# Head products of a graph network on TensorE: four blocks of 256 columns, or seven block products of 128

## The chip, the core and the metric

The kernel runs on one core of a Trainium2 chip. The core has five engines that run side by side, each through its own fixed list of instructions: TensorE (PE, matrix products, with a separate weight load, PEld), VectorE (DVE), ScalarE (ACT), GpSimd (POOL) and SyncE (SP, which here issues every DMA). Data sits in SBUF, 128 partitions wide. Products land in PSUM, which has 8 banks, each with room for 512 f32 numbers in each partition. [...]what TensorE computes is taken out by ACT or DVE. The metric is the device time of one execution in microseconds: the median of three runs.

## The reference

There are 128 graphs of 64 nodes, each node with 512 features in f32, and one adjacency matrix. Four layers follow, each adding its result to x and normalizing over the features:

```
x = layernorm(x + L0(x))    # deg*(x Wi^T + b) + adj x Wj^T
x = layernorm(x + L1(x))    # 4 attention heads, elu; output attention with W_out, elu; FFN; layernorm
x = layernorm(x + L2(x))    # one attention: softmax(mask(leaky(e_src + e_dst))) (x W2)
x = layernorm(x + L3(x))    # the same with W3
```

A head computes `attn (x W_h)`, with W_h of 512 x 512; the kernel uses that it equals `(attn x) W_h`. Layers 2 and 3 are done in the same way. All products are in f32.

## The kernel before

**Tiling.** The 8192 tokens (nodes of all graphs) are taken 256 at a time: 32 "pairs" p of T = 2 token tiles of 128 tokens, and a token tile holds two graphs. For each pair, Python generators write out the stages: `stage_first` (layer 0), `stage_scores` (attention weights of the heads, and y = attn x for each head, transposed, by half-height matmuls named yp), `stage_heads` (y W_h, elu, kept as hT), `stage_project` (hT W_out, named who), `stage_out` (output attention, elu, FFN, layer norm), and `stage_gat` twice (layers 2 and 3).

**The order.** A queue at the end of the kernel (lines 1081 to 1113) gives each stage a due time in units of `TURN` = 107 us per pair and advances the generators by the times that they yield. That gives each step a rank. `Plan.order` (lines 205 to 297) then makes a list schedule from a cost per instruction (`cost`, line 317) with waits between engines, and plays it out: each engine gets a fixed order of instructions (all issued at line 304, so the profile names line 304 for nearly everything). A tile pool has a fixed number of buffers per tag; a step that opens a tile waits until a buffer of the tag is free. All PSUM tiles share one tag of 8 buffers, one bank each. `with nc.soon()` puts what empties PSUM ahead of other work.

**Products.** Layer 0 (from pair 4 on), the projection, the second FFN matrix and layers 2, 3 use `strassen` (line 586): a 2 x 2 block product with seven block products in place of eight. Its left blocks (tokens, two token tiles by two halves of the contraction) are the stationary operand, the right blocks (weights, 256 columns) move. Sums of left blocks are made on POOL (`sums`, line 649). Sums of right blocks are made once: for layer 0 and W_out they are stored in DRAM and each block is loaded for each use (`stage_stream`, `part_from`, a ring "ws" of 4 buffers of 512 KB); for w2, W2 and W3 all seven blocks stay in SBUF (`stage_resident`, line 560). Two PSUM tiles, stx and sty, take the results in turn; DVE adds them to the result. At most two such units run at a time (line 593).

The heads do not use it. For each head, four output blocks of 128 features: the weight block is stationary, and all 256 tokens of the pair move:

```
hp[:, c, :, :], lhsT=w_h[h][:, k, ts(2 * q + c, P)],
rhs=y[:, k, h % 2, :, :].rearrange("p t i -> p (t i)"),
```

Two output blocks share a PSUM bank, and `elu` (line 772) takes the bank out by two ACT operations and one on DVE.

**Layers 2 and 3.** The products of attention and x, transposed (gp, line 1042), use half-height matmuls: for each graph 64 tokens are the contraction, x is stationary and the 64 columns of its attention move. ACT and DVE then bring the results into gT, with one sum.

**Scores.** The head scores of pair 0 are made on TensorE (transposed x, then the products fp with the score weights); for other pairs DVE makes them by dot products with rows that DMAs spread over the partitions.

Of the kernel before, what the change touches and what calls it, by code (L numbers as in the profile page):

```python
# [28 lines left out]
NWS = 4  # L29
AHEAD = 4  # L30
# [286 lines left out]
def cost(engine, name, args, kw, out):  # L317

    size = max(math.prod(v.shape[1:]) for v in out) if out and isinstance(out[0], View) else 512
    if engine == "tensor":  # L320
        if name == "transpose":
            return size * 0.00085, 0.0

        beside = P * P // math.prod(kw["lhsT"].shape)
        return size * (0.00169, 0.00106, 0.0, 0.00053)[beside - 1], 0.0
# [10 lines left out]
def gnn_stack_kernel(  # L336
# [124 lines left out]

    was = {}
    score = {}

    def score_weights(Ws, avecs, name):
# [3 lines left out]
        for h in range(n):  # L469
            for s in range(2):  # L470
                for c in range(KC):
# [4 lines left out]
                    )  # L476
            yield 5.0
# [15 lines left out]
    for p in range(1, AHEAD):  # L493
        xs[p] = load_x(p)
    w_h, a_h = [], []
    for h in range(H):
        w_h.append(weight(W_heads[h], D, f"wh{h}"))
        a_h.append(
            rows([a_heads[h, ts(s, D)] for s in range(2)], f"a_{h}", ["who", "o", "A", "A"][h])
        )  # L500
    beta_sb = row(beta, "beta")
# [6 lines left out]
    PARTS = ("21", "11", "T1", "T2", "22", "T3", "T4")  # L508

    def sums_of(parts, b12):  # L510

        add = lambda out, a, b, op: nc.gpsimd.tensor_tensor(out, a, b, op)
        add(parts["T1"], b12, parts["11"], ALU.subtract)
        add(parts["T2"], parts["22"], parts["T1"], ALU.subtract)
        add(parts["T3"], parts["22"], b12, ALU.subtract)
        if "T4" not in parts:
            parts["T4"] = parts["11"]
        add(parts["T4"], parts["21"], parts["T2"], ALU.subtract)
# [3 lines left out]
    def stage_stream(src, name):  # L522

        parts = {}
        for q in ("11", "12", "21", "22"):
            i, j = int(q[0]) - 1, int(q[1]) - 1
            parts[q] = unit.tile([P, KC, D // 2], FP, tag="ws", bufs=NWS, name=f"raw_{name}_{q}")
            nc.sync.dma_start(
                out=parts[q],
                in_=src[ts(i, D), ts(j, D // 2)].rearrange("(c p) o -> p c o", p=P),  # L530
# [4 lines left out]
        def store(q):  # L535
            d[q] = dp.tile([P, KC, D // 2], FP, tag=f"d_{name}_{q}", name=f"d_{name}_{q}")
            nc.sync.dma_start(out=d[q], in_=parts[q])
# [3 lines left out]
        parts["T1"] = unit.tile([P, KC, D // 2], FP, tag="who", name=f"T1_{name}")  # L541
        parts["T2"] = unit.tile([P, KC, D // 2], FP, tag="o", name=f"T2_{name}")
        parts["T3"] = parts["12"]
        sums_of(parts, parts["12"])
        for q in ("T1", "T2", "T3", "T4"):
            store(q)
# [3 lines left out]
    def part_from(name, p):  # L550

        def part(q):
            t = unit.tile([P, KC, D // 2], FP, tag="ws", bufs=NWS, name=f"ws_{name}_{p}_{q}")
# [3 lines left out]

    resident = {}

    def stage_resident(src, name):  # L560

        w = wp.tile([P, len(PARTS), KC // 2, D // 2], FP, tag=f"r_{name}", name=f"r_{name}")
        parts = {q: w[:, i, :, :] for i, q in enumerate(PARTS)}
        b12 = unit.tile([P, KC // 2, D // 2], FP, tag="s3", bufs=2, name=f"b12_{name}")
        for q in ("11", "12", "21", "22"):
            i, j = int(q[0]) - 1, int(q[1]) - 1
            nc.sync.dma_start(
                out=b12 if q == "12" else parts[q],
                in_=src[ts(i, D // 2), ts(j, D // 2)].rearrange("(c p) o -> p c o", p=P),
            )  # L570
        yield 4.0
        sums_of(parts, b12)
        resident[name] = lambda q: parts[q]
        yield 0.0
# [11 lines left out]
    def strassen(A, B, S, R, kc, name, gap, fresh=False, whole=lambda t: None):  # L586
# [6 lines left out]
        while no >= 2 and no - 2 not in ended:  # L593
            yield 1.0
        s1, s2, s3, s4 = S(name)
        R = R.rearrange("p t (h o) -> p (t h) o", h=2)
        half = D // 2
        x = psum.tile([P, half], FP, tag="b", name=f"stx_{name}")
        yz = psum.tile([P, 2, half], FP, tag="b", name=f"sty_{name}")

        def product(ps, a, q, first, last):
            b = B(q)
            with nc.together():
                for k in range(kc):
                    nc.tensor.matmul(
                        ps, lhsT=a[:, k, :], rhs=b[:, k, :], start=(first and k == 0),
                        stop=(last and k == kc - 1), skip_group_check=True,
                    )
# [12 lines left out]
        product(yz[:, 0, :], A(1, 0), "21", True, False)  # L621
        yield gap
        product(x, A(0, 0), "11", True, False)
        put(x, R[:, 0, :])
        yield gap
        s4(A(1, 0))
        product(yz[:, 1, :], s1, "T1", False, False)
        if fresh:
            add(yz[:, 0, :], R[:, 0, :])
            put(yz[:, 1, :], R[:, 3, :])  # L630
        else:
            add(yz, R[:, 0:4:3, :])
        yield gap
        product(x, s2, "T2", False, False)
        put(x, R[:, 1, :])
        yield gap
        product(yz[:, 1, :], A(1, 0), "22", False, True)
        add(yz[:, 1, :], R[:, 1, :])
        whole(0)
        yield gap  # L640
        product(x, s3, "T3", False, False)
        add(x, R[:, 3, :])
        yield 2 * gap
        product(x, A(1, 1), "T4", False, True)
        put(x, R[:, 2, :])
        whole(1)
        ended.add(no)

# [129 lines left out]


# [4 lines left out]
    outs = {}  # L784
# [381 lines left out]
```

## Time and profile before

| | |
|---|---|
| median of three runs | 3453.69 us (3453.62 to 3456.76) |
| the profiled execution: time, and span from first to last instruction | 3457.33 us, 3455.5 us |
| mean granted TensorE clock | 0.987 |
| PE, PEld, DVE, ACT, POOL busy | 3381.8, 2878.7, 2424.6, 997.7, 1444.6 us |
| moved by DMA | 540 MB, 156 GB/s in the mean, 47.3% of the 16 DMA engines |
| costliest group on PE: head products hp | 4096 records, 951.8 us busy |

How to read the profile's lines. A group line names the line of the code, engine, operation, the tiles (written<-read, numbers left out), partitions x elements, the count, then busy time, mean ns of one, and idle time of the engine before it with what ended it. In a timeline line the first number is the start in us from the span's start, the second the length to the last end, and consecutive equal instructions are merged (x8). For matmuls the pair "128*128 128x256" gives the stationary block and what is moved through it. An f32 matmul appears as two records, a transposition as one. Matmuls overlap: a record lasts longer than the distance to the next one, so the sum of records is not the work. The chain that ended last is followed back from the last instruction through what released each one.

### The profile page before, as it was taken

To read this page: it belongs to the slowest core of one execution; us is meant where nothing else is said; L and a number is where in the kernel's file an instruction comes from. 1 tells how busy PE (TensorE), PEld (TensorE's weight loads), DVE (VectorE), ACT (ScalarE), POOL (GpSimd) and SP (SyncE) were. 2 spreads that over 40 slices of the span, in tenths; PEclk is the share of its full clock that TensorE was granted. 3 is DMA by queue.
4 is the path that set the end of the run, shared out by engine and by line. 5 is a ranking of instruction groups with operands and counts; after the bars stand their busy time and mean duration, and the time that the engine had idled before them with its cause. 6 is when DMAs were issued, how large, how long until landed. Compare 5 with 4: busy or idle time off the path is not lost.

```text
span 3455.5 us, 52610 instructions
## 1 busy us (share of the span) xinstructions
PE 3381.8 (98%) x19228; PEld 2878.7 (83%) x19228; DVE 2424.6 (70%) x5408; ACT 997.7 (29%) x2536; POOL 1444.6 (42%) x1528
## 2 busy tenths in 40 slices
PE   8899999999999999999999999999999999999986
PEld 4788888888888888888888888888888888888875
DVE  7757766777667777677777677777677777677755
ACT  1233223232233232233232233232232232232221
POOL 5424344444344444344444344444344444344322
PEclk9999999999999999999999999999999999999987
DMA  8834444444454444444445454445444445444420
GB/s 310 269 110 141 159 154 151 153 159 160 154 169 147 158 159 159 153 165 149 159 156 165 150 166 146 160 155 167 154 159 152 156 153 169 153 158 147 136 87 31
DMA packets 203761, 540.38 MB, mean 156 GB/s; under 512 B 21824, under 2 KB 31088, under 8 KB 203504
## 3 DMA queue, kind: packets, MB, share of 16 engines
q1 hardware_dynamic: 203504, 537.02, 47.3%
q8 instruction: 154, 2.52, 0.3%
q14 instruction: 103, 0.84, 0.1%
HBM read 509.12 MB, written 27.81 MB: 155 GB/s over the span
## 4 chain that ended last, share of the span: by engine, by line
PE 94%; DVE 4%; POOL 1%; issue 1%; DMA 1%; ACT 0%; SPq 0%; POOLq 0%; ACTq 0%; DVEq 0%
PE hp L304 25%; PE stx_o L304 13%; PE stx L304 12%; PE sty_o L304 10%; PE sty L304 9%; PE hidp L304 7%; PE gp L304 4%; PE yp L304 3%; PE stx_y L304 3%; PE sty_y L304 2%; PE axp L304 2%; PE bc L304 1%; PE op L304 1%; DVE x L304 1%; PE oTp L304 1%
## 5 line engine op out<-in xcount | busy, mean ns | idle before, releaser
L304 PE MATMUL hp<-ys,wh 128*128 128x256 f32 x4096 | 951.8, 381 | 0.0
L304 PEld LDWEIGHTS hp<-ys,wh 128*128 128x128 f32 x4096 | 765.2, 190 | 109.2 <-issue 2.1
L304 DVE CUSTOM_DVE_ANT_0 j<-x,rows 128x512 bf16<-128x512 f32 x752 | 613.8, 816 | 76.6 <-DMA rows<-d_h 66.5
L304 ACT ACTIVATE hT<-hp 128x512 f32<-128x512 f32 x256 | 152.5, 596 | 866.1 <-PE hp L304 865.7
L304 POOL TENSOR_SCALAR rs<-mv 128x1 f32<-128x1 f32 x256 | 104.5, 408 | 620.5 <-DVE mv L304 591.2
L304 DVE TENSOR_SCALAR x<-x,mv,rs 128x512 f32<-128x512 f32 x256 | 213.2, 833 | 106.5 <-POOL rs L304 106.4
L304 DVE SCALAR_TENSOR_TENSOR hT<-hT,hp 128x512 f32<-128x512 f32 x256 | 175.1, 684 | 143.7 <-ACT hT L304 139.6
L304 DVE TENSOR_TENSOR x<-stx,x 128x256 f32<-128x256 f32 x368 | 154.9, 421 | 156.1 <-PE stx L304 152.7
L304 PE MATMUL sty_o<-ws_wo,hT 128*128 128x256 f32 x1024 | 247.7, 385 | 1.4 <-DMA ws_wo<-d_wo 1.4
L304 PE MATMUL stx_o<-ws_wo_T,s_o 128*128 128x256 f32 x1024 | 245.7, 383 | 2.8 <-DVE e L304 2.1
L304 PE MATMUL hidp<-oT,w 128*128 128x256 f32 x1024 | 237.6, 382 | 0.7 <-ACT oT L304 0.7
L304 PEld LDWEIGHTS sty_o<-ws_wo,hT 128*128 128x128 f32 x1024 | 189.6, 190 | 51.4 <-issue 22.3
L304 PEld LDWEIGHTS stx_o<-ws_wo_T,s_o 128*128 128x128 f32 x1024 | 192.3, 190 | 31.6 <-DVE e L304 2.5
L304 PEld LDWEIGHTS hidp<-oT,w 128*128 128x128 f32 x1024 | 190.1, 190 | 28.8 <-ACT oT L304 0.9
L304 PE MATMUL sty<-r_W,gT 128*128 128x256 f32 x768 | 202.2, 387 | 1.7 <-ACT gT L304 1.7
L304 ACT COPY ys<-yp 128x512 f32<-128x512 f32 x256 | 131.7, 600 | 176.4 <-PE yp L304 171.6
L304 DVE BATCH_NORM_STATS2 st<-x 128x6 f32<-128x512 f32 x256 | 176.8, 691 | 6.4
L304 DVE TENSOR_TENSOR who<-stx_o,who 128x256 f32<-128x256 f32 x160 | 66.9, 418 | 156.2 <-PE stx_o L304 156.1
L304 POOL TENSOR_TENSOR rs<-rs,mhalf 128x1 f32<-128x1 f32 x256 | 160.8, 628 | 21.3
L304 PEld LDWEIGHTS sty<-r_W,gT 128*128 128x128 f32 x768 | 148.5, 194 | 23.9 <-ACT gT L304 2.4
L304 ACT ACTIVATE hT<-hT 128x512 f32<-128x512 f32 x256 | 161.4, 630 | 8.2
L304 POOL TENSOR_TENSOR hid<-hid 128x256 f32<-128x256 f32 x32 | 32.2, 1005 | 306.3 <-ACT hid L304 299.8
(170 smaller groups left out, 6225.3 us busy)
## 6 DMA issues: line engine op xcount, KB each, us to landing
ws_wo_T<-d_wo_T SPq DMA_DIRECT2D x256, 512.0 KB, 3.4
ws_wo<-d_wo SPq DMA_DIRECT2D x192, 512.0 KB, 3.4
rows<-d_h SPq DMA_DIRECT2D x248, 256.0 KB, 4.2
ws_w_T<-d_w_T SPq DMA_DIRECT2D x112, 512.0 KB, 3.3
ws_w<-d_w SPq DMA_DIRECT2D x84, 512.0 KB, 3.1
rows<-d SPq DMA_DIRECT2D x128, 256.0 KB, 3.9
rows_1o<-in_a_out_dram SPq DMA_DIRECT2D x64, 256.0 KB, 3.4
out_dram<-x SPq DMA_DIRECT2D x64, 256.0 KB, 2.0
```

Source lines behind the costliest of these rows:

```text
L304: getattr(getattr(self.tc.nc, s.engine), name)(*map(real, args), **{k: real(v) for k, v in kw.items()})
```

## The change

**Heads.** A general `seven` is split out of `strassen`: the schedule of the seven block products and of emptying PSUM, with the block product itself handed in. `strassen` uses it as before. The heads now use it too, with weight blocks stationary and token blocks moving: the 512 x 512 head matrix is cut into 2 x 2 blocks of 256 x 256, the result likewise into two halves of features by two token tiles. Each block product is 4 matmuls with a stationary 128 x 128 block and 128 columns moving. Sums of weight blocks are made once at the start, in place in SBUF (`head_sums`); sums of token blocks on POOL after each y tile (t1, t2, and one in place), and one per head (`t4`). The results are copied out by ACT (four per head) and added by DVE (three per head) into hT, and then `elu_of` applies the elu to each half of hT, with a PSUM tile as scratch. Up to `UNITS` = 3 units of seven products run at a time.

**Weights.** The seven blocks of w2, W2 and W3 are no longer kept in SBUF: they are stored in DRAM at the start and loaded for each use, through a ring "wk" of 6 buffers of 256 KB. The seven blocks of layer 0 are prepared later than before.

**Layers 2 and 3.** The attention of a token tile is written into a tile aTg of 128 x 128 with zeros between the two graphs (two such tiles, filled with zeros once), so that gp becomes full-height matmuls with 128 columns moving, one PSUM tile per token tile.

**Scores.** Pair 1 makes its head scores on TensorE as pair 0 does. The planner's cost of half-height matmuls is changed.

```diff
+NWK = 6
+UNITS = 3
...
-        return size * (0.00169, 0.00106, 0.0, 0.00053)[beside - 1], 0.0
+        return (
+            size * 0.00169 if beside == 1 else 0.208 / beside + 0.0003 * size
+        ), 0.0
...
+    aTg = [cp.tile([P, T, P], FP, tag=f"aTg{i}", name=f"aTg{i}") for i in range(2)]
+    for aT in aTg:
+        nc.gpsimd.memset(aT, 0.0)
...
+        w = wp.tile([P, KC // 2, 7, D // 2], FP, tag=f"wh{h}", name=f"wh{h}")
...
+    RINGS = {D: ("ws", NWS), D // 2: ("wk", NWK)}
+
+    def head_sums(w):
+
+        a11, a21, a12, a22, s2, s3, s4 = (w[:, :, i, :] for i in range(7))
+        nc.gpsimd.tensor_tensor(a21, a21, a22, ALU.add)
+        nc.gpsimd.tensor_tensor(s2, a21, a11, ALU.subtract)
+        nc.gpsimd.tensor_tensor(s3, a22, s2, ALU.subtract)
+        nc.gpsimd.tensor_tensor(s4, a12, s2, ALU.subtract)
...
+    def part_from(name, p, K=D):
+
+        ring, bufs = RINGS[K]
 
         def part(q):
-            t = unit.tile([P, KC, D // 2], FP, tag="ws", bufs=NWS, name=f"ws_{name}_{p}_{q}")
+            t = unit.tile([P, K // P, D // 2], FP, tag=ring, bufs=bufs, name=f"ws_{name}_{p}_{q}")
             nc.sync.dma_start(out=t, in_=streams[name][q])
             return t
         return part
-
-    resident = {}
-
-    def stage_resident(src, name):
...
+    def seven(product, R, shape, name, gap, fresh=False, once=lambda: None, whole=lambda t: None):
...
-        while no >= 2 and no - 2 not in ended:
+        while no >= UNITS and no - UNITS not in ended:
             yield 1.0
+        x = psum.tile([P, *shape], FP, tag="b", name=f"stx_{name}")
+        yz = psum.tile([P, 2, *shape], FP, tag="b", name=f"sty_{name}")
+        y, z = yz[:, 0], yz[:, 1]
...
+        product(0, y, True, False)
+        yield gap
+        product(1, x, True, False)
+        put(x, R(0, 0))
+        yield gap
+        once()
+        product(2, z, False, False)
+        if fresh:
+            add(y, R(0, 0))
+            put(z, R(1, 1))
+        else:
+            add(yz, R(None, None))
+        yield gap
+        product(3, x, False, False)
+        put(x, R(0, 1))
+        yield gap
+        product(4, z, False, True)
+        add(z, R(0, 1))
+        whole(0)
+        yield gap
+        product(5, x, False, False)
+        add(x, R(1, 1))
+        yield 2 * gap
+        product(6, x, False, True)
+        put(x, R(1, 0))
+        whole(1)
+        ended.add(no)
...
+    def elu_of(x, name):
+
+        ps = psum.tile(x.shape, FP, tag="b", name=f"elu_{name}")
+        with nc.soon():
+            nc.scalar.activation(ps, x, AF.Relu, scale=-1.0)
+            nc.scalar.activation(ps, ps, AF.Exp, scale=-1.0)
+            nc.vector.scalar_tensor_tensor(x, ps, -1.0, x, ALU.add, ALU.max)
...
-        if p == 0:
+        if p < 2:
...
+            Y = lambda k, t: y[:, 2 * k : 2 * k + 2, :, t, :]
...
+            nc.gpsimd.tensor_tensor(t1, Y(0, 1), Y(0, 0), ALU.subtract)
+            nc.gpsimd.tensor_tensor(t2, Y(1, 1), t1, ALU.subtract)
+            nc.gpsimd.tensor_tensor(Y(0, 1), Y(1, 1), Y(0, 1), ALU.subtract)
+            yh.append((y, t1, t2))
...
-            for q in range(KC // 2):
-                hp = psum.tile([P, 2, T, P], FP, tag="b", name=f"hp_{p}_{h}_{q}")
...
+            def product(i, ps, first, last):
+                a = w[:, :, (2, 0, 1, 4, 6, 5, 3)[i], :]
+                b = (Y(1, 0), Y(0, 0), t1, t2, Y(1, 1), Y(0, 1), Y(1, 0))[i]
+                with nc.together():
+                    for c in range(2):
+                        for k in range(2):
                             nc.tensor.matmul(
-                                hp[:, c, :, :], lhsT=w_h[h][:, k, ts(2 * q + c, P)],
-                                rhs=y[:, k, h % 2, :, :].rearrange("p t i -> p (t i)"),
-                                start=(k == 0), stop=(k == KC - 1),
+                                ps[:, c, :], lhsT=a[:, k, ts(c, P)], rhs=b[:, k, :],
+                                start=(first and c == 0 and k == 0),
+                                stop=(last and c == 1 and k == 1), skip_group_check=True,
                             )
-                elu(hT[:, 2 * q : 2 * q + 2, :, :], hp)
-                yield TURN / H / 2
+
+            def t4():
+                nc.gpsimd.tensor_tensor(Y(1, 0), Y(1, 0), t2, ALU.subtract)
+
+            yield from seven(
+                product, lambda i, j: hT[:, 2 * i : 2 * i + 2, j, :], [2, P], f"h_{p}_{h}",
+                TURN / H / 8, True,
+                t4,
+                lambda i: elu_of(hT[:, 2 * i : 2 * i + 2, :, :], f"{p}_{h}_{i}"),
+            )
...
-            A, resident["w2"], sums(A, KC // 2, nc.gpsimd), o, KC // 2, f"y_{p}", 1.8,
+            A, part_from("w2", p, D // 2), sums(A, KC // 2, nc.gpsimd), o, KC // 2, f"y_{p}", 1.8,
...
-        aT = unit.tile([P, T, N], FP, tag="aT", bufs=2, name=f"aT_{name}_{p}")
+        aT = aTg[used.pop()]
...
+        for t in range(T):
+            ps = psum.tile([P, 2, KC // 2, P], FP, tag="b", name=f"gp{name}_{p}_{t}")
+            with nc.together():
+                for c in range(KC):
+                    nc.tensor.matmul(
+                        ps[:, c // 2, c % 2, :], lhsT=x[:, t, ts(c, P)], rhs=aT[:, t, :],
+                        start=True, stop=True,
+                    )
...
-    start(-0.55 * TURN, 0, stage_stream(W0T, "w0"))
-    start(-0.3 * TURN, 0, stage_stream(W_out[0 : 2 * D, :], "wo0"))
-    start(-0.1 * TURN, 0, stage_stream(W_out[2 * D : 4 * D, :], "wo1"))
-    start(0.2 * TURN, 0, stage_resident(w2, "w2"))
...
+    start(0.6 * TURN, 0, stage_stream(W0T, "w0"))
+    start(-0.55 * TURN, 0, stage_stream(W_out[0 : 2 * D, :], "wo0"))
+    start(-0.3 * TURN, 0, stage_stream(W_out[2 * D : 4 * D, :], "wo1"))
+    start(0.2 * TURN, 0, stage_stream(w2, "w2"))
+    start(1.0 * TURN, 0, stage_stream(W2, "W2"))
...
+    start(1.3 * TURN, 0, stage_stream(W3, "W3"))
```

## The prediction

> **What bounds the kernel now.** I read the page's busy times first, then the chain that ended last, then the busy time by stretch.
>
> ```profile
> PE 3381.8 (98%) x19228; PEld 2878.7 (83%) x19228; DVE 2424.6 (70%) x5408; ACT 997.7 (29%) x2536; POOL 1444.6 (42%) x1528
> ...
> PE 94%; DVE 4%; POOL 1%; issue 1%; DMA 1%; ACT 0%; SPq 0%; POOLq 0%; ACTq 0%; DVEq 0%
> ```
>
> ```profile
> 0.00:172.00 172.00, 142.61 (x674) 97.12 (x675) 126.66 (x234) 35.24 (x70) 87.96 (x72) 0.94 0.84 291
> 172.00:1200.00 1028.00, 1024.67 (x5894) 881.03 (x5893) 719.23 (x1603) 310.78 (x782) 421.83 (x448) 1.00 0.47 151
> 1200.00:2200.00 1000.00, 1000.00 (x5761) 861.73 (x5760) 716.59 (x1615) 297.29 (x759) 423.22 (x451) 1.00 0.48 157
> ...
> 3369.00:3455.00 86.00, 57.46 (x253) 44.67 (x253) 45.94 (x116) 9.79 (x41) 23.35 (x37) 0.72 0.09 31
> ```
>
> The columns after the length are busy us of PE, PE's weight loads, DVE, ACT, POOL, then granted clock, DMA share, GB/s. Between 172 and about 3280 us TensorE is never idle, at full clock, while DVE is at 70-72%, DMA at 47%. There only TensorE's own time counts. Ahead of it lies a start and behind it a tail in which PE waits on chains of other engines. But a busy PE says little of its rate, since matmuls overlap, so I take the rate from starts in the timeline. Every f32 matmul in the code makes two records ("passes").
>
> ```profile
> 1475.05 2.06 PE L304 MATMUL yp<-aT,x 64*128 64x128 f32 x32
> 1476.94 1.06 PE L304 MATMUL axp<-aggr,x 64*128 64x128 f32 x16
> ...
> 1530.20 1.04 PE L304 MATMUL oTp<-ident,o 128*128 128x128 f32 x8
> ...
> 1538.09 1.89 PE L304 MATMUL sty_o<-ws_wo_T,hT 128*128 128x256 f32 x8
> 1539.91 2.00 PE L304 MATMUL gp<-aT,x 64*128 64x64 f32 x32
> 1541.85 3.72 PE L304 MATMUL hidp<-oT,w 128*128 128x256 f32 x16
> ```
>
> A merged row runs from its first start to its last end. sty_o: 8 passes of 256 columns take 1.89 with one mean pass (385 ns in the groups) at the end: (1.89-0.385)/7 = 215, so 216 ns a pass, the median of start differences too. The heads are 4096 such passes (hp in the groups below), 885 us, a quarter of the chain.
>
> **The head matmuls.** Before, a head is 4 output blocks x 4 contraction blocks x 256 columns = 16 matmuls, 32 passes. After, it is 7 products x 4 matmuls of 128 columns = 28 matmuls, 56 passes; over 32 x 4 heads 7168 passes. One eighth of the multiplying goes, but each 128x128 weight block now serves 128 columns, not 256, so the passes rise by 1.75. The question is what a pass of 128 columns costs with a new full weight block each. No row has this exact form. Bounds and nearest rows:
>
> - By moving alone: oTp, a transposition of 128 columns, (1.04-0.273)/7 = 109 ns.
> - By loading alone: the score matmuls of pair 0 move 8 columns per 128x128 load, and 15 loads took 1.75 us:
>
> ```profile
> 75.25 1.75 PEld L304 LDWEIGHTS fp<-wa_h,x1T 128*128 128x128 f32 x15 [0.24 <-issue]
> ```
>
> (1.75-0.19)/14 = 111 ns a load.
>
> - Both overlapped: axp (and yp) move 128 columns per load of 128 columns, in two half-height arrays side by side. axp's 16 passes are 8 such pairs; the two of a pair start 7 ns apart, and a pass lasts 0.272 (its median), so the row of 1.06 us leaves (1.06-0.007-0.272)/7 = 0.112 from pair to pair: each half array does a full load and a full move every 112 ns.
> - Not overlapped at all: 109+111 = 220 ns, 1577 us. axp excludes it for half arrays, and hp's 216 for loads under 256 columns.
>
> Here the Trainium skill speaks against the change ("TensorE: Matmul & The Clock Gate", Back-to-back issue gap): in a real stream of load and matmul pairs 128 columns sustain about 81 ns, against 56 for the matmul alone in 16-bit, since both set the spacing. If these 25 ns came on top of 109 here, a pass would cost 134, the heads 961 us, and the kernel would be 158 us above my sum. I take axp's 112, which is of this chip, this type and the same ratio of loading to moving: 7168 x 0.112 = 803 us. **-82 us.**
>
> **Full rows in layers 2 and 3.** gp is 32 half-height passes of 64 columns now; 16 full passes of 128 later. From the rows: after sty_o's 8 x 216 = 1728 ns gp could start at 1539.82 and starts at 1539.91, and it lasts 1.94 until hidp instead of 16 x 112 = 1.79. So 1.79 us of work, the same by the new form (16 x 112), and 0.09+0.15 of change of array shape, which falls away: 64 x 0.24 = **-15 us**. Zeros written once at the start (two memsets) are hidden in POOL's idle time.
>
> **Scores of pair 1 on PE**: 8 transpositions x 109 and 16 passes x 112: **+2.7 us**; DVE loses 16 dot products of (816+80) ns, 14 us, SP 8 row loads.
>
> **What goes to the other engines**, all beside PE if it stays in time:
>
> ```profile
> L304 DVE CUSTOM_DVE_ANT_0 j<-x,rows 128x512 bf16<-128x512 f32 x752 | 613.8, 816 | 76.6 <-DMA rows<-d_h 66.5
> ...
> L304 ACT COPY who<-stx_o 128x256 f32<-128x256 f32 x96 | 35.4, 369 | 103.6 <-PE stx_o L304 103.3
> ...
> L304 DVE TENSOR_TENSOR x<-stx,x 128x256 f32<-128x256 f32 x368 | 154.9, 421 | 156.1 <-PE stx L304 152.7
> ...
> L304 POOL TENSOR_TENSOR gT<-gT,s 128x256 f32<-128x256 f32 x64 | 58.0, 906 | 28.7 <-PE sty L304 28.1
> ```
>
> - Emptying PSUM per head: three DVE adds (128 x 3 x 0.421 = 162 us) and four ACT copies (128 x 4 x 0.369 = 189). The ELU keeps its three operations per half head.
> - DVE in layers 2, 3: one add of 256 columns for two of 128: 64 x 0.42 - 128 x 0.29 = -10.
> - POOL: three sums of 512 columns per y tile (like s_o<-hT, 1.42 us) x 64 = 273 us, one of 256 per head (0.9) x 128 = 115, head weight sums 16 x 1.4 = 22. The stream and resident sums only change places.
> - DVE with two SBUF inputs stretches beside POOL: j<-x,rows has a median of 691 ns, a maximum of 2236, a mean of 816, 94 us lost; x<-x,mv,rs (546 median, 833 mean) 73; x<-o,rs_1i,x (737 at least, 1619 mean) 56. These 223 us grow with POOL's large sums, some 1.3 times: +67.
>
> DVE: 2425+162-10-14+67 = 2630, 78% of the new span; ACT 1187, 35%; POOL 1855, 55%. None becomes the bound by sum.
>
> **Weights from DRAM.** 7 blocks x 3 matrices x 32 pairs = 672 loads of 256 KB, 176 MB more: 716 MB, 212 GB/s, about 63% of the DMA engines. SP's issue takes 0.32 us (its own rows in the trace), 215 us more on a queue that mostly waits for buffers. What hides them is the depth of the ring. For the present 644 block loads I matched issue with first use: at least 4.2 us, median about 18, against 3.4 us to landing. Six small buffers at 1.8 us a product give about 9. Cover gone, each late block would cost up to its landing, 3 us. I count 0.
>
> **New waits.** Within a head, the fourth product adds onto the PSUM region that the second filled, so PE waits until ACT has copied it out; the sixth and seventh do the same through ACT and DVE. Behind a waiting product stands all of PE's fixed order. Today the same pattern exists in 188 units (64+28+32+64) and PE waits on DVE about 7 us in it (stx<-x 5.1, stx_y<-o 1.0, stx_o<-who 0.5). 128 more units at this rate give 5; with DVE at 78% I double it: **+10 us** (bounds 0 and 65, half a us per head). On POOL, the y sums stand ahead of the layer-norm roots (rs), for which DVE's x<-x,mv,rs waits; that is 1.4-4 us, inside a turn of 100.
>
> **Start and tail.** The first heads have little other work to fill PE: y's sums on POOL (4 us) against the 1.8 us of the two products that need none, and the seventh product right behind the add of the sixth, about 1 us x 4: **+6**. In the tail the first token tile of gp is copied while the second is multiplied: some 1.3 us of copies hidden, three times: **-4**.
>
> **Sum**: -82-15+2.7+10+6-4 = -82. The profiled execution took 3457.33 us with a span of 3455.5; the median is 3453.69, 3.6 lower. Span 3373, median **3372 us**, 2.4% faster.
>
> **Rivals.**
> A. A full-array pass costs more than 112. It is slower than before from 112 + 82/7.168 = 123 ns on; at 134, 3530 us. For it: the skill's pairs, and that no row loads and moves 128 columns in one full array. Against it: axp's row.
> B. The waits within a head bind: half a us per head more than counted gives 3372+64 = 3436. For it: DVE's stretches to 1.7-2.2 us stand ahead of the adds in its order, and PSUM has 8 banks with a head now holding two all the time. Against it: the margins that the plan leaves today, mostly 2-6 us from an emptied region to the product that reuses it.
> C. Streams late: one block in ten by 1 us is 67 us, 3440. Against it: the lead of 4-18 us.
> D. The other way: the pass at 109 and no added wait, 3372-21-10 = 3341.
>
> **Chances.** The likeliest 0.70 (its own range 3350 to 3395), A 0.10, B 0.11, C 0.04, D 0.05. Of B and C about 0.03 reaches past no change (0.2%, 7 us, is what three runs can tell). Faster 0.86, same 0.02, slower 0.12. The range leaves A out and takes in B's half us per head: 3340 to 3436.
>
> **What would show it.** PE's timeline: head products of 8 passes spaced 112 ns (0.90 us start to start); 123 or more refutes the sum. gp as x8 full passes without a gap around it. DVE busy near 2630, POOL near 1850, DMA near 0.6. In the chain of waits PE should still hold above 90%; waits of PE's head rows on ACT or DVE, or on wk blocks by DMA, above 30 us would make B or C right.

## The result, and the profile after

| | before | after |
|---|---|---|
| median, us | 3454.55 (3453.62 to 3456.76) | 3404.85 (3403.24 to 3406.36) |
| ratio after / before | | 0.9855, 95% interval 0.9838 to 0.9872 |
| span of the profiled execution | 3455.5 | 3402.6 |
| granted TensorE clock, mean | 0.987 | 0.989 |

The kernel became 50 us faster, where 82 was forecast. The time lies inside the forecast range, but 33 us above the forecast and 10 above the likeliest case's own range (3350 to 3395). The sign was right; four tenths of the gain went elsewhere. The rest of this document looks for them.

The page after, busy times and the chain that ended last:

```profile
PE 3285.9 (97%) x21300; PEld 2898.4 (85%) x21300; DVE 2655.5 (78%) x5696; ACT 1163.7 (34%) x2924; POOL 1771.1 (52%) x1866
PE 76%; DVE 16%; DMA 3%; POOL 3%; issue 2%; SPq 1%; ACT 0%; POOLq 0%; DVEq 0%; ACTq 0%
```

The busy sums are close to what was forecast (DVE 2630, ACT 1187, POOL 1855). The chain is not: TensorE holds 76% of it instead of 94%, and DVE 16% instead of 4%. Something on DVE has begun to end last, though it is busy 78% of the time.

The busy time by stretch, with the columns that the prediction explains (PE, its loads, DVE, ACT, POOL, granted clock, DMA share, GB/s):

```profile
0.00:172.00 172.00, 138.28 (x817) 98.58 (x818) 125.53 (x212) 42.50 (x93) 126.64 (x102) 0.91 0.80 277
172.00:1200.00 1028.00, 1010.15 (x6636) 899.33 (x6635) 796.29 (x1720) 366.91 (x922) 529.61 (x558) 1.00 0.65 211
1200.00:2200.00 1000.00, 991.21 (x6527) 884.87 (x6527) 805.09 (x1732) 353.06 (x881) 527.51 (x560) 1.00 0.66 214
```

Before, PE was busy 1000.00 of 1000 us in the third row. Now 9 us of 1000, and 18 of 1028 (3 before), are idle at full clock. And the head products, in PE's timeline:

```profile
1475.58 1.05 PE L306 MATMUL sty_h<-t,wh 128*128 128x128 f32 x8
1476.47 1.06 PE L306 MATMUL stx_h<-t,wh 128*128 128x128 f32 x8
1477.36 1.06 PE L306 MATMUL sty_h<-t,wh 128*128 128x128 f32 x8
1478.26 1.06 PE L306 MATMUL stx_h<-t,wh 128*128 128x128 f32 x8
```

Starts lie 0.89 to 0.90 us apart for 8 passes: 112 ns a pass, exactly the number that the heads were costed with.

**An account of the loss.** To see where the rest went I gave every PE record its undisturbed distance to the next one (216 ns for a 256-column pass, 112 for a 128-column pass with a new block, 112 for a pair of half-height passes, 109 for a transposition, 429 for 512 columns or for four quarter-size passes side by side) and summed. A stretch minus this nominal work is the stretch's loss; in the start and the tail, where the granted clock was 0.72 to 0.94, the lower clock counts as loss too. "Middle" runs from 180 us to 60 us before the last head product; within it I part the losses at 0.2 us a gap: above, PE waits for somebody; below, it is changes of array shape and the like.

| us | before | after | difference |
|---|---|---|---|
| nominal work | 3272.3 | 3193.0 | -79.3 |
| lost in the first 180 us | 43.3 | 47.1 | +3.8 |
| middle, losses up to 0.2 us | 64.0 | 47.7 | -16.3 |
| middle, gaps over 0.2 us (how many) | 5.3 (10) | 53.3 (93) | +48.0 |
| lost in the tail | 70.8 | 61.6 | -9.2 |
| span | 3455.5 | 3402.6 | -52.9 |

The work shrank as forecast. The new waits, counted at +10, appear as +48 in the gaps. PE's waits between 172 and 3230 us, the largest, as us in total, times, longest:

```profile
PE yp L306 <- DVE who L306: 11.1, 12, 1.3
PE sty_y L306 <- DMA ws_w<-d_w: 4.1, 6, 1.2
PE pt L306 <- DVE e L306: 3.9, 8, 0.8
PE bc L306 <- DVE f L306: 3.1, 1, 3.1
PE stx_y L306 <- DVE o L306: 3.0, 7, 0.4
...
PE stx_h L306 <- DVE hT L306: 1.9, 2, 1.1
```

Before, this list (from 172 to 3283 us) had three lines and 3.4 us:

```profile
PE bc L304 <- DVE f L304: 2.5, 1, 2.5
PE stx_o L304 <- issue: 0.7, 1, 0.7
PE stx_y L304 <- DVE o L304: 0.2, 1, 0.2
```

The list holds only what PE's queue is seen to wait for, so it is shorter than the 53 us. By starts, the last passes of a yp group, which need a bank to be emptied, lose some 15.7 us in 24 gaps; the transposition pt, which waits for the softmax's result, loses 7.8 in 19; and the products of w2 after axp lose about 10. The new products themselves (stx_h, sty_h) hardly wait. One instance shows the make of it; all engines around 748 us:

```profile
746.74 1.26 POOL L306 TENSOR_TENSOR s<-ax 128x512 f32<-128x512 f32 x1
746.80 1.48 DVE L306 TENSOR_SCALAR x<-x,mv,rs 128x512 f32<-128x512 f32 x1
...
748.07 1.33 POOL L306 TENSOR_TENSOR s<-ax,s 128x512 f32<-128x512 f32 x1
...
748.41 1.55 DVE L306 SCALAR_TENSOR_TENSOR o<-o,mv_1i,rows_gamma 128x512 f32<-128x512 f32 x1
...
749.88 0.41 DVE L306 TENSOR_TENSOR who<-sty_o,who 128x256 f32<-128x256 f32 x1
...
750.35 0.97 PEld L306 LDWEIGHTS yp<-aT,x 64*128 64x128 f32 x16 [0.26 <-DVE who L306]
```

yp's last 16 passes need the PSUM bank that the who add empties. The product in it ended at 747.4 us (sty_o started at 745.51 and lasted 1.89). The add, behind two long DVE instructions in DVE's fixed order, starts at 749.88. The two lie beside POOL sums and take 1.48 and 1.55 us; the shortest of their kinds in this trace take 0.51 and 0.74.

This instance costs PE only 0.2 us, the dearest of the 24 cost 1.5. All 24 are alike: from the end of the product to the start of the add DVE stands idle for at most 0.07 us, and its instructions there run 1.08 to 1.79 us longer than the shortest of their kinds, in each case more than PE loses (0.21 to 1.49). So at yp DVE itself is late, not a result that it waits for. That suggests a cause, and others compete with it: POOL's own lateness, DVE's greater load, the number of units and PSUM banks, a bad static order, late streams. The runs take them one at a time.

### The profile page after: what moved, and what is told of

Same layout as the page of the kernel before. It is cut to its first block, busy times and chain, and to the rows that moved or that the text cites. A ratio compares the mean times of both kernels' runs of the same rounds, so it can differ in the third digit from the quotient of the medians.

```text
span 3402.6 us, 59449 instructions
## 1 busy us (share of the span) xinstructions
PE 3285.9 (97%) x21300; PEld 2898.4 (85%) x21300; DVE 2655.5 (78%) x5696; ACT 1163.7 (34%) x2924; POOL 1771.1 (52%) x1866
## 3 DMA queue, kind: packets, MB, share of 16 engines
q1 hardware_dynamic: 302208, 716.63, 64.5%
## 4 chain that ended last, share of the span: by engine, by line
PE 76%; DVE 16%; DMA 3%; POOL 3%; issue 2%; SPq 1%; ACT 0%; POOLq 0%; DVEq 0%; ACTq 0%
PE stx_h L306 13%; PE stx L306 11%; PE stx_o L306 11%; PE sty_h L306 10%; PE sty L306 9%; PE hidp L306 6%; PE sty_o L306 5%; DVE e L306 4%; PE gp L306 3%; DVE x L306 3%; DVE o L306 2%; PE stx_y L306 1%; PE yp L306 1%; DVE st_1i L306 1%; PE sty_y L306 1%
## 5 line engine op out<-in xcount | busy, mean ns | idle before, releaser
L306 DVE CUSTOM_DVE_ANT_0 j<-x,rows 128x512 bf16<-128x512 f32 x736 | 636.3, 864 | 51.5 <-DMA rows<-d_h 42.5
L306 PE MATMUL stx_h<-ys,wh 128*128 128x128 f32 x3072 | 402.8, 276 | 8.0 <-DVE hT L306 7.9
L306 PEld LDWEIGHTS stx_h<-ys,wh 128*128 128x128 f32 x3072 | 386.2, 192 | 28.0 <-issue 7.3
L306 ACT COPY hT<-stx_h 128x256 f32<-128x256 f32 x384 | 142.5, 372 | 571.9 <-PE stx_h L306 562.7
L306 DVE TENSOR_SCALAR x<-x,mv,rs 128x512 f32<-128x512 f32 x256 | 222.0, 867 | 72.4 <-POOL rs L306 72.1
L306 PE MATMUL sty_h<-ys,wh 128*128 128x128 f32 x2048 | 274.0, 277 | 0.0
L306 PEld LDWEIGHTS sty_h<-ys,wh 128*128 128x128 f32 x2048 | 254.3, 192 | 7.1
L306 POOL TENSOR_TENSOR ys<-ys,t 128x256 f32<-128x256 f32 x128 | 111.9, 877 | 252.0 <-PE sty_h L306 251.8
L306 ACT ACTIVATE elu<-hT 128x512 f32<-128x512 f32 x256 | 154.1, 602 | 224.8 <-DVE hT L306 220.3
L306 DVE SCALAR_TENSOR_TENSOR hT<-elu,hT 128x512 f32<-128x512 f32 x256 | 174.9, 684 | 16.3 <-ACT elu L306 14.7
L306 DVE TENSOR_TENSOR x<-sty,x 128x256 f32<-128x256 f32 (+1 forms) x184 | 102.1, 555 | 81.6 <-PE sty L306 81.1
```

The lines of the kernel that those rows point to most:

```text
L306: getattr(getattr(self.tc.nc, s.engine), name)(*map(real, args), **{k: real(v) for k, v in kw.items()})
```

## The experiments

**One part alone: old heads, with streams and full rows.**

```diff
-UNITS = 3
+UNITS = 2
...
+            for q in range(KC // 2):
+                hp = psum.tile([P, 2, T, P], FP, tag="b", name=f"hp_{p}_{h}_{q}")
...
+                elu(hT[:, 2 * q : 2 * q + 2, :, :], hp)
+                yield TURN / H / 2
-            yield from seven(
```

> The changed kernel with the heads as before (16 matmuls of 256 columns, their way out of PSUM, no sums for them, at most two units): what is left of the change is the streamed blocks and the full rows. By the sum of the prediction the full rows alone give -15 and streaming costs nothing: 3440. If late blocks are what ate the gain, it stays at 3450 to 3460 with waits of TensorE on DMA.

Measured: 3417.12 us (3415.98 to 3419.78), ratio 0.9889 (0.9872 to 0.9905), 23 us below what was expected. So the streams from DRAM and the full rows alone give 37 of the 50 us, and the heads only 12. Gaps over 0.2 us: 3.7 us in 5. The 176 MB of added loads cost nothing that shows, and the waits come with the heads. By account, the heads on top of this kernel bring -81.9 of nominal work, then +14.9 at the start, +53.4 in the middle and +0.6 in the tail: more than four fifths of their gain goes straight back, most of it in the middle.

**Full rows taken back** (only gp in half-height form, as before; everything else as after).

```diff
-        aT = aTg[used.pop()]
+        aT = unit.tile([P, T, N], FP, tag="aT", bufs=2, name=f"aT_{name}_{p}")
...
+            for c in range(KC):
+                for t in range(T):
+                    for b in range(2):
+                        nc.tensor.matmul(
+                            ps[b][:, c // 2, c % 2, t, :], lhsT=x[ts(b, N), t, ts(c, P)],
```

> The changed kernel with gp of layers 2 and 3 as before, in half-height passes of 64 columns. The prediction's term for the full rows was -15 us, all of it from changes of array shape, so 3420 here; if the run with the old heads is a guide (22 us less lost in the middle than the kernel before), 3427.

Measured: 3453.59 (3451.09 to 3457.73), ratio 0.9994 (0.9985 to 1.0002): undoing the full rows takes back the whole gain, 49 us, where 15 to 22 was expected. With the new heads and the streams, but without the full rows, the kernel is no faster than before. By account 24 of these are losses up to 0.2 us (71.9 for 47.7), some 0.4 us for each of 64 gp groups where 0.24 was forecast; 13 lie in the tail, 11 are gaps over 0.2 us, a size that another static order alone can make (below). The old-heads kernel gives the same small losses a second way: 43.9 there for 64.0 before, 0.31 us a group.

The starts in the trace of before show what the 0.24 left out. It holds what is lost ahead of gp and up to the next group. But that next group loses as well:

```profile
1539.91 2.00 PE L304 MATMUL gp<-aT,x 64*128 64x64 f32 x32
1541.85 3.72 PE L304 MATMUL hidp<-oT,w 128*128 128x256 f32 x16
1545.40 1.89 PE L304 MATMUL stx_o<-ws_wo_T,s_o 128*128 128x256 f32 x8
```

The 16 passes of hidp take 3.55 us where 16 x 216 ns is 3.46: its second pass starts 0.10 us late. The same delay follows 63 of the 64 gp groups of before. With it a group costs 0.34 us (0.09 ahead, 0.14 inside and at its end, 0.10 behind it), 22 us in all.

**The amount of DVE's work.** The dot products run on 64 of 512 columns, and the plan still costs them in full, so every order is the same. Seven eighths of the dot products are left out.

```diff
+            if args and isinstance(args[0], View) and args[0].tile in NARROW:
+                return [a[:, 0:64] if isinstance(a, View) else a for a in args]
...
                 junk = unit.tile([P, D], BF, tag="junk", name=f"j_{name}_{s}_{t}")
+                NARROW.add(junk.tile)
```

> The changed kernel with the attention dot products on VectorE cut from 512 to 64 columns (the scores are then other numbers); every engine keeps the same instructions in the same order. Theory 1 (VectorE, at 78%, runs behind the fixed order and TensorE waits for it): VectorE's busy time falls from 2656 to about 2250 us, TensorE's gaps in the middle stretch (54 us in gaps of over 0.2 us) fall below 20, the time falls by 30 to 40 us to about 3365. Theory 2 (blocks from DRAM arrive late) and theory 3 (too few PSUM banks by the order itself): gaps stay above 40, time above 3390.

Measured: 3382.97, one execution. The page, and the first wait of PE:

```profile
PE 3278.8 (97%) x21300; PEld 2895.3 (86%) x21300; DVE 2241.2 (66%) x5696; ACT 1164.3 (34%) x2924; POOL 1633.1 (48%) x1866
```

```profile
PE yp L313 <- DVE who L313: 8.6, 12, 0.9
```

DVE lost 414 us of busy time, more than the 230 that it is above before, and is at 66%. Yet the gaps stay at 43.7 us in 76, and yp waits for who the same twelve times. The time fell by 22 us, of which the gaps give 10, the tail 9 and the start 3. The load of DVE is not what makes most of the waits.

**The amount of POOL's work**, in the same way: POOL's in-place sums on 16 columns; most of each sum is left out.

```diff
+            if s.engine == "gpsimd" and len(args) > 2 and isinstance(args[2], View):
...
+                    if out.shape[-1] >= 128:
...
+                            a, (slice(None),) * (len(a.shape) - 1) + (slice(0, 16),)
```

> The changed kernel with GpSimd's in-place sums cut to 16 columns in the last dimension (results are then other numbers), same order on every engine. If what delays VectorE is mainly that GpSimd's sums block it: VectorE's busy time falls by some 200 us with its own work unchanged, its long dot products return to 0.69 us, and TensorE's gaps fall below 25 us, time about 3370. If it is VectorE's own work: busy time falls less than 100, gaps stay above 40.

Measured: 3350.19, one execution, 55 us less than after. Gaps 19.5 us in 30.

```profile
PE 3269.6 (98%) x21300; PEld 2893.9 (86%) x21300; DVE 2439.3 (73%) x5696; ACT 1162.9 (35%) x2924; POOL 1155.5 (35%) x1866
```

POOL does a third less, and DVE, with unchanged work, is 216 us less busy. So POOL matters. This doesn't say how: by finishing its own results late, or by holding DVE up.

**Only the sums that the change added** (from pair 1 on: two sums of each y tile replaced by a memset, the in-place ones cut to 16 columns; those sums are left out).

```diff
+                if p > 0:
+                    (NARROW if a.shape[-1] == P and a.tile is y.tile else BLANK).add(a)
+                nc.gpsimd.tensor_tensor(a, b, c, ALU.subtract)
```

> The changed kernel with the sums that the change adds on GpSimd for each y tile and each head taken down from pair 1 on (t1 and t2 become a memset, which reads nothing, the two in-place sums are cut to 16 columns; results are then other numbers), same order on every engine. Theory after the first runs: GpSimd's sums block VectorE's instructions that read two SBUF operands, VectorE frees PSUM late, TensorE waits. If the added sums are the cause: gaps of over 0.2 us in the middle fall from 53 to below 25 us, time 3365 to 3380. If GpSimd's older sums do the harm where VectorE's added work has moved: gaps stay above 40, time 3390 to 3400.

Measured: 3396.96, one execution; gaps 50.1 us in 74. The added sums aren't the ones that do most of it. The next run, which takes the reads of the older sums away as well, leaves 12 us of gaps; so, by subtraction, most harm comes from sums that were there before, such as that of 746.74 us above (layer 0's). That the new order has put beside them DVE work that PE waits for is seen in the instances at yp and argued for the rest.

**POOL present but blind.** Each POOL sum of 256 or 512 columns becomes three memsets of its output. It writes as much, takes longer in all, and reads nothing; all these sums are left out. If POOL's lateness costs the time, the waits stay; if its reads do, they go. PE, DVE and ACT run the same instructions in the same sequence as in the changed kernel.

```diff
+                    if (
+                        s.engine == "gpsimd" and name == "tensor_tensor"
+                        and math.prod(args[0].shape[1:]) in (256, 512)
...
+                        for _ in range(3):
+                            self.tc.nc.gpsimd.memset(args[0].real(), 0.0)
+                        continue
```

> The changed kernel with every sum of token blocks and every bias sum on GpSimd (256 or 512 columns) replaced by three memsets of the same output: 3 x 0.52 or 3 x 0.32 us, a little longer than the sums (1.4 and 0.9 us in the mean), but nothing is read; the results are zeros. Same order on every engine, GpSimd as late as before or later. If GpSimd's reads block VectorE and this makes TensorE wait: VectorE's dot products and norms return to 0.69 and 0.55 us in the mean, its busy time falls by about 250 us, gaps of over 0.2 us in the middle fall from 53 to below 20, time 3340 to 3365. If the cause is that GpSimd itself is late (its roots and sums come late to the others): gaps stay above 40 and the time at 3390 to 3410.

Measured: 3349.35 (3348.23 to 3350.47), ratio 0.9691 (0.9663 to 0.972); gaps 11.7 us in 19. First the page and groups of this run, then the same groups of the changed kernel:

```profile
PE 3268.1 (98%) x21300; PEld 2899.0 (87%) x21300; DVE 2306.3 (69%) x5696; ACT 1163.1 (35%) x2924; POOL 1920.0 (57%) x4210
...
L314 DVE CUSTOM_DVE_ANT_0 j<-x,rows 128x512 bf16<-128x512 f32 x736 | 505.4, 687 | 57.4 <-DMA rows<-d_h 48.5
L314 DVE SCALAR_TENSOR_TENSOR hT<-elu,hT 128x512 f32<-128x512 f32 x256 | 175.0, 684 | 22.2 <-ACT elu L314 20.6
L314 DVE TENSOR_SCALAR x<-x,mv,rs 128x512 f32<-128x512 f32 x256 | 163.6, 639 | 95.8 <-POOL rs L314 95.1
L314 DVE SCALAR_TENSOR_TENSOR x<-o,rs_1i,x 128x512 f32<-128x512 f32 x64 | 47.4, 740 | 28.6 <-POOL rs_1i L314 28.4
```

```profile
L306 DVE CUSTOM_DVE_ANT_0 j<-x,rows 128x512 bf16<-128x512 f32 x736 | 636.3, 864 | 51.5 <-DMA rows<-d_h 42.5
...
L306 DVE TENSOR_SCALAR x<-x,mv,rs 128x512 f32<-128x512 f32 x256 | 222.0, 867 | 72.4 <-POOL rs L306 72.1
...
L306 DVE SCALAR_TENSOR_TENSOR hT<-elu,hT 128x512 f32<-128x512 f32 x256 | 174.9, 684 | 16.3 <-ACT elu L306 14.7
...
L306 DVE SCALAR_TENSOR_TENSOR x<-o,rs_1i,x 128x512 f32<-128x512 f32 x64 | 84.0, 1313 | 2.8 <-POOL rs_1i L306 2.4
```

POOL is busier than in the changed kernel (1920 for 1771), and still the time falls by 55 us, 42 of them gaps: this speaks against POOL's own lateness as the main cause. One thing isn't held fixed: a memset waits for no input. Counted by PE's passes, the blind sums end in the median one pass later than in the changed kernel, but one in ten ends 25 passes or more earlier. The roots (rs), for which DVE waits most on POOL, aren't earlier in the median, and DVE waits for them longer than before. At yp, moreover, DVE wasn't waiting for anybody. Nor does the data of zeros bring a faster clock: the granted mean is 0.990 for 0.989.

DVE is 349 us less busy for the same 5696 instructions. The dot product falls from 864 to 687 ns, x<-o,rs_1i,x from 1313 to 740, x<-x,mv,rs from 867 to 639. hT<-elu,hT, whose one operand lies in PSUM, stays at 684 in both, and so does x<-stx,x (419 and 420). This is what the Trainium skill says ("SBUF — State Buffer", Who interferes with whom): a DVE instruction with two SBUF inputs contends with a GpSimd instruction that reads SBUF, not with one that only writes. x<-x,mv,rs has one SBUF tensor as input and is stretched all the same. The same section says that tensor_scalar contends when it runs in a two-port mode; that would fit, and also that its mean under memsets is still 639 against a median of 558, but no run here separates it. PE's waits in this run:

```profile
PE sty_y L314 <- DMA ws_w<-d_w: 5.1, 7, 1.1
PE bc L314 <- DVE dg L314: 1.1, 1, 1.1
...
PE yp L314 <- DVE who L314: 0.3, 1, 0.3
```

yp's wait for who has gone from 11.1 to 0.3 us. What is left of the waits is mostly the one stream that is late.

**One of the blocked instructions moved.** The layer norms' last step goes to ACT, with the bias made on POOL; the result is the same.

```diff
-        nc.vector.tensor_scalar(x, x, mean, rstd, ALU.subtract, ALU.mult)
+        nb = small.tile([P, 1], FP, tag="nb", name=f"nb_{name}")
+        nc.gpsimd.tensor_scalar(nb, mean, rstd, -1.0, ALU.mult, ALU.mult)
+        nc.scalar.activation(x, x, AF.Identity, bias=nb, scale=rstd)
```

> The changed kernel with the last step of each layer norm, (x - mean) * rstd, moved from VectorE (256 x 0.867 us, an instruction stretched from 0.546 by GpSimd) to ScalarE as one activation with scale and bias per row; GpSimd makes the bias, one more small instruction. By the theory: VectorE's busy time falls by 220 us, gaps in the middle to about 30 us, time about 3380. Rival: VectorE's load is not the cause and the chain of the norm grows by about 0.5 us: 3400 to 3415.

Measured: 3392.64 (3388.66 to 3403.72), ratio 0.9827 (0.9809 to 0.9846). It takes 222 us of the stretched instruction off DVE for 208 on ACT (815 ns each).

```profile
PE 3287.1 (97%) x21300; PEld 2903.8 (86%) x21300; DVE 2407.0 (71%) x5440; ACT 1353.5 (40%) x3180; POOL 1842.2 (54%) x2122
```

Gaps are 32.1 us in 51. The largest wait is a new one:

```profile
PE sty_h L306 <- POOL t L306: 7.6, 10, 1.6
```

The median is 12 us below the changed kernel's, though the intervals of the two ratios overlap a little. The gaps fell as expected (to about 30), the time did not reach 3380; it lies between the two cases that were expected. It is the fastest kernel here that leaves no work out. With the bias made elsewhere than on POOL it wasn't tried.

**The planner's costs.** Vector instructions, dot products, roots, short matmuls and DMA issues are costed at their measured durations.

```diff
-        return 0.06, 0.0015 * size
+        return 0.32, 0.0015 * size
     if name == "tensor_tensor_reduce":
-        return 0.78, 0.0
+        return 0.95, 0.0
...
+        size = max(math.prod(v.shape[1:]) for v in views)
+        inside = not any(v.tile.pool.space is PSUM for v in views)
+        return 0.17 + (0.00135 if inside and size >= 512 else 0.00103) * size, 0.0
```

> The changed kernel with the planner's cost per instruction set to the durations of the trace (statistics 0.69 us where it had 0.18, dot products 0.95 for 0.78, roots on GpSimd 0.64 for 0.25, DMA issue 0.32 for 0.06, a pass of 128 columns 112 ns). All work is the same, only the order differs. Theory 1: the order now leaves VectorE its time, gaps fall from 54 to below 30 us, time 3365 to 3390. If the load itself is the cause, or the blocks from DRAM: within 10 us of 3405, either way.

Measured: 3488.12 (3487.04 to 3489.98), ratio 1.0093 (1.0078 to 1.0109): slower than before. The gaps are 93.9 us in 135, at other places; the losses up to 0.2 us are up by 30 and the tail by 11:

```profile
PE gp L306 <- ACT aTg L306: 21.2, 26, 0.9
PE pt L306 <- ACT elu L306: 12.5, 12, 1.1
```

The expectation failed. Means closer to the truth made a worse order. Why this order is worse stays open; a mean cannot say which of two sums will meet, but that is argued, not shown.

**Units of seven at a time, 2 and 4 for 3.**

```diff
-UNITS = 3
+UNITS = 2
```

> The changed kernel with at most two units of seven products at a time instead of three. Theory 3 (PSUM banks are short, since each unit holds two of eight): the waits of TensorE for banks go, 3385 to 3395. By the blocking theory the number of units is no cause, and with the heads always holding one of them the other products queue: 3410 to 3440.

> The changed kernel with up to four units of seven products at a time. If the collapse with two units came from units queueing for each other, and three is enough, four gives the same within 10 us of 3405; if queueing still costs with three, 3380 to 3395; if PSUM banks are the shortage, slower than 3415.

With 2: 3743.96, ratio 1.0833 (1.0817 to 1.0849), 300 us above either case that was expected; gaps some 355 us in 480.

```profile
PE stx_y L306 <- DVE o L306: 68.3, 24, 3.7
PE oTp L306 <- DVE o L306: 50.5, 26, 2.9
```

That the heads nearly always hold one unit, so that the other products queue for the second, is argued and not shown. With 4: 3434.97 (3433.09 to 3438.41), ratio 0.9939 (0.9923 to 0.9956), gaps 72.8 us in 75, the largest 26.0 on bc<-f, with 11.8 on the w2 stream. By the expectation a time above 3415 would speak for a shortage of PSUM banks; but +20 us of gaps is a size that another order alone can make (below), so the run doesn't decide it. Three is the best of the three, and neither more units nor fewer are a way out.

**Streams.** One kernel gives w2 a ring of its own (3 buffers, 3 for W2 and W3), another restores the early preparation of layer 0's blocks.

```diff
...
-        ring, bufs = RINGS[K]
+        ring, bufs = RINGS[K] if K == D else (("wk", 3) if name == "w2" else ("wl", 3))
```

```diff
-    start(0.6 * TURN, 0, stage_stream(W0T, "w0"))
-    start(-0.55 * TURN, 0, stage_stream(W_out[0 : 2 * D, :], "wo0"))
-    start(-0.3 * TURN, 0, stage_stream(W_out[2 * D : 4 * D, :], "wo1"))
+    start(-0.55 * TURN, 0, stage_stream(W0T, "w0"))
+    start(-0.3 * TURN, 0, stage_stream(W_out[0 : 2 * D, :], "wo0"))
+    start(-0.1 * TURN, 0, stage_stream(W_out[2 * D : 4 * D, :], "wo1"))
```

> The changed kernel with the six small buffers for streamed blocks split: three for the blocks of w2, three for those of W2 and W3. In the trace the blocks of W2 and W3 are fetched 20 to 50 us ahead and sit in the shared ring, the blocks of w2 are fetched only 5 to 7 us ahead, and TensorE waits for them about 10 us in all, in the y products. If the shared ring is why, the gaps ahead of the y products vanish and the time falls by about 10 to 3395; if three buffers are too few for 1.8 us a product, waits on DMA grow and it is 3410 or more.

> The changed kernel with the blocks of layer 0 prepared first again (the order of the three large streams as before the change). Start: in the changed kernel 47 us are lost in the first 180, with the old heads 32; at 137 to 144 us the sums of these blocks on GpSimd (2.5 us each) hold up VectorE and TensorE waits 5.1 us. If moving the stream behind the first heads did this, the start loss falls by 5 us or more, time 3395 to 3400; if the sums only move in front of the first scores: the same or up to 10 us slower.

Own ring: 3434.19 (3431.91 to 3440.2), ratio 0.9936 (0.9922 to 0.9951). The waits on DMA ahead of w2's products fall to 1.9 us, but this is another static order, with 64.0 us of gaps in all (sty_h<-t 11.7, bc<-f 11.6) and a tail of 73.5. So neither case that was expected came true: the waits on DMA fell and the time rose. Early preparation: 3406.17 (3403.61 to 3408.83), ratio 0.9853 (0.9838 to 0.9867), as the changed kernel and as the second case expected; 51.7 us are lost at the start for 47.1.

Taken together: edits that make the planner find another order move the gaps by 10 to 40 us (half rows +11, own ring +11, 4 units +20, costs +41, norm on ACT -21). A result of such a run within that size says little of its mechanism, and the norm's gain may be in part a luckier order. The old heads are another order too, so the size of what the heads bring is measured for these two orders only. The narrow and the blind kernels keep the order, and the verdict on POOL's reads rests on them.

## Why the prediction was right in sign and short by 33 us

Taken by runs, the heads brought 12 us where -82, +10 and +6 make 66, and the other parts 37 where -15, +2.7 and -4 make 16. That the sum fell into the range is in part luck: one part gave much less than forecast and the other more.

**The heads, -82.** Right to the nanosecond: 7168 passes at 112. Rival A (123 ns and above) is refuted; the 134 that was estimated from the Trainium skill ("TensorE: Matmul & The Clock Gate", Back-to-back issue gap) isn't there. Taking axp's row, two half arrays side by side, for a full array was the right choice.

**Full rows, -15.** Too small: 16 in the comparison of the two kernels, 20 to 24 where the part is done or undone alone, and 13 more in the tail, where -4 was counted. The term took the gap on either side of one gp group, 0.24, and missed the 0.10 us inside the group behind it; the trace of before has 0.34 a group. That is 22 us; what the two runs gain beyond it lies in the tail, in the start and in the order.

**Scores of pair 1, +2.7.** The nominal work of the old-heads kernel is 2.6 above before.

**New waits, +10.** This is the step that failed: +48. It was counted from the waits that before already has, 188 units and 7 us, doubled. Neither half holds. Of the 7 us, 5.9 lie in the tail and 0.5 in the first 172 us; in the long stretch between, which the term was for, there are 0.2. And the new waits don't belong to the new units: head rows wait little, and PE stops instead at yp, pt and w2's products. And the doubling stood for DVE's load, which isn't what makes them: cutting it to 66% leaves 44 of the 53 us. What most of them need is POOL's reads: without these, 12 are left. The prediction had DVE's stretch beside POOL (223 us today, 67 more), and booked it as busy time, "None becomes the bound by sum". The sum was right to 1%, 2656 for 2630, in part by luck: counted over the fastest twentieth of each form, the stretch grew by 138 us, not 67, while the instructions overlap more. And a stretch is not spread out: at 748 us it is some 0.9 and 0.8 us one after the other, ahead of the one add whose bank PE needs.

What stays open is why the order with the old heads stands the same kind of reads with 3.7 us of gaps. It has 1388 us of POOL and 5312 DVE instructions, the changed one 1771 and 5696, and PE does the heads in 82 us less; but the added sums alone cost 3 us of gaps, and the dot products' load 10. The traces show where the orders differ: of the 288 DVE adds into who, which empty the projection's banks, 6 start more than 2 us after their product with the old heads, 33 before, 56 in the changed kernel and 6 in the blind one; the stretch that stands ahead of these adds comes to 45, 69, 118 and 10 us. That the added copies and adds took the room which the old order had for a stretch is argued, not shown.

**Rival B** asked for waits within a head, from DVE's stretches "ahead of the adds in its order". Its cause was right and its place wrong: waits on the heads' rows of more than 30 us, named as its sign, did not come. Its time (3436) was as far off on the other side, 31 us, as the forecast's 33.

**Streams, 0.** Nearly right. The lead of about 9 us was too high for w2: some 6 us in the median from issue to first use, against 4.3 to 4.8 us to landing, and PE waits some 5 us on them in the records. W2 and W3 lead by some 35 us. DMA came to 64.5% for 63%. Rival C, with 67 us, is refuted.

**Start and tail, +6 and -4.** +4 and -9. The +4 hides two larger numbers: the other parts take 11 off the start, which was not predicted, and the heads put 15 on it. Two waits at the start are a pt that waits 10.5 us for the first softmax on DVE (8.5 with the old heads), and a head row that waits 5.1 for hT; the rest of the 15 is not traced.

**The chain.** "PE should still hold above 90%" failed, 76%. It was the sharpest sign in the profile that the term for waits, not the rate of passes, was off.

**Layer-norm roots behind POOL's sums**, was called harmless inside a turn, and is: in the blind run DVE waits 95.1 us for rs, more than the 72.1 of the changed kernel, and PE doesn't feel it.

## What to carry to other kernels

When TensorE is bound by its rate and runs a fixed order, cost a change in two columns: the passes, from distances between starts, and the delays at the places where another engine frees what the next pass needs. An engine that is busy 78% by sum can still be late at each such place, above all where its instructions are stretched by a neighbour; look in the timeline at what stands ahead of each instruction that empties PSUM. To separate "does too much", "is late" and "blocks its neighbour", keep the order and change one of them: shorten the work, or replace it by work that takes as long and reads nothing.

## What the runs showed of the hardware that was not expected

- 128 columns moving with a new full 128 x 128 f32 block each cost 112 ns a pass, though loading takes 111 and moving 109: the two overlap fully, in a stream of 7168.
- POOL sums that read SBUF stretch DVE's instructions with SBUF operands by 26% to 77% in the mean (864 for 687, 1313 for 740 ns); memsets on POOL, busy longer, leave the dot product at 687, about its median of 691 before. In this kernel taking the reads away saved DVE 349 us of busy time, and the whole kernel 55.
- A group of half-height matmuls between full ones costs 0.34 us beyond its work: 0.09 ahead of it, 0.14 inside and at its end, and 0.10 at the second pass of the group behind.
